# Quarter swaps of convolution weights as DMA transfers, and a re-ordered preparation cycle

## The chip, the cores and the metric

The kernel runs on one core of one Trainium2 chip. The metric is the device time of one execution in microseconds (us). TensorE (PE in the profile) multiplies, VectorE (DVE), ScalarE (ACT) and GpSimd (POOL) work on elements, and SyncE (SP) issues nearly all of the DMA transfers, one after the other from a single queue.

## The reference, cut to what matters

Four residual layers work on x of shape (4, 32, 32, 16): two position-dependent convolutions, one interval-pooling layer, and one more convolution of the same kind. Each normalizes its input first (`_gn`). The time goes to the three convolutions:

```python
first = jnp.einsum('ijyx,byxc->bijc', Msq, inputs)
kern = jnp.transpose(G, (0, 1, 5, 4, 2, 3)).reshape(h * w * f, c, 3, 3)
shifted = lax.conv_general_dilated(x_nchw, kern, (1, 1), 'SAME')   # h*w*f output channels
diff = jax.nn.relu(inputs[:, None, None, :, :, :] - shifted)
second = jnp.einsum('ijyx,bijyxc->bijc', Wsq, diff)
return first - second
...
x = x + _L0_conv_ref(_gn(x), L0_conv_M, L0_conv_W, L0_conv_G)
```

Every output position (i, j) and feature f has its own 3x3x16 kernel in G, so the convolution has 32 * 32 * 16 output channels, and its result is consumed at once by the relu and the weighted sum.

## The kernel before, in words

**Phases, chunks, steps.** Three convolution layers times two pairs of images make six phases. A phase has eight chunks of 128 output positions, a chunk 32 steps (16 features times 2 images), so there are 1,536 steps. A step is a group of matmuls into a pair of PSUM banks, a scaling of them by ScalarE (L663), more matmuls, and one VectorE instruction that applies the relu, multiplies with W and sums (L680). The matmuls of a step are split: `first_part` of step S is issued before `second_part` of step S-1.

**Units.** Weights come in units of four features (`FU`), 192 units u in all, each used by eight steps: unit u is first used at step 8u. To keep fp32 precision on the matmul path, a weight is split into a high part (its upper bits) and a low part. A prepared unit is a tile `parts` of 128 partitions x 2 x 3 x 512 elements: `WU`, `WL`, `WD` for slot 0, and the same three for slot 1, which is slot 0 with its upper and lower 64 partitions exchanged. A second tile, `W9`, holds the ninth tap. There are three buffers of each (`AHEAD + 1`) and two of the raw weights (`RAWS`). The first two units go another way (`prep_plain`).

**Preparation.** The generator `prep_parts` prepares one unit per cycle of eight steps; each `yield` ends a step. For unit u: VectorE masks the raw weights to the high part (`upper`, L203); ScalarE makes `W9` (L175), `WD` (L236) and `WU` (L240); GpSimd subtracts to get `WL` (L237), adds to `W9` (L238) and `WD` (L241), swaps quarters of 32 partitions with four copies (L243, L245), and then subtracts the identity tap from the next unit's raw weights (`prep(u + 1)`, L214), in place. Two transfers from SBUF to SBUF (L251) fill slot 1 from slot 0; the text calls these two the exchange. Then `load_raw` (L110) fetches the raw weights of unit u + 2.

**Other work in the same queues.** The generator `behind` runs what the next phase needs: the norm (`group_norm`), eight small transfers of the normalized image to DRAM (xs<-xt, L381), 24 that read it back as shifted rows (raw<-xs, L392), and `place`, a block of 12 transfers for each of two images (L298, L300), called a placing block here. In the middle of the run it also runs the interval layer. What a step of `prep_parts` yields says whether `behind` may go on in it where it asks for an `IDLE` or a `CALM` step.

**What sets the order.** The schedule is manual: each engine runs its instructions in the order in which the program issues them, and waits on semaphores for data. SP too: a transfer that has to wait holds all that were issued behind it. In `conv_layer`, each step first takes one step of `prep_parts`, then issues its matmuls, and then, if allowed, one piece of `behind`.

Of the kernel before, what the change touches and what calls it, by code (L numbers as in the profile page):

```python
# [8 lines left out]
F32 = mybir.dt.float32  # L9
F32R = mybir.dt.float32r  # L10
I32 = mybir.dt.int32
AF = mybir.ActivationFunctionType
ALU = mybir.AluOpType
AX = mybir.AxisListType

P = 128
# [5 lines left out]
NP = H * H  # L22
# [11 lines left out]
FU = 4  # L34
# [3 lines left out]
HIGH = -(1 << 12)  # L38
# [6 lines left out]
def net_kernel(ctx: ExitStack, tc: tile.TileContext, x, xq, xi, convs, iv_w, iv_b, out):  # L45
# [26 lines left out]
    nc = tc.nc  # L72
    ctx.enter_context(tc.manual_schedule())

    const = ctx.enter_context(tc.tile_pool(name="const", bufs=1))
    wpool = ctx.enter_context(tc.tile_pool(name="wpool", bufs=2))
    work = ctx.enter_context(tc.tile_pool(name="work", bufs=1))
# [20 lines left out]
    IDLE = 0  # L98
    CALM = -1
# [6 lines left out]
    def load_raw(u):  # L106
        if u < n_chunks * NU:
            n = u // NU
            raws[u] = wpool.tile([P, 3, FU, P], F32, tag="raw", bufs=RAWS, name=f"raw_{u}")
            nc.sync.dma_start(raws[u], convs[phases[n // NT][1]][2][n % NT, u % NU])  # L110
# [55 lines left out]
    def rows_mask(name, view):  # L166

        m = const.tile([P, 2], F32, name=name)
        nc.vector.tensor_reduce(m[:, 0:1], view, axis=AX.XYZ, op=ALU.add)
        nc.vector.tensor_scalar(m[:, 1:2], m[:, 0:1], -2.0, 1.0, op0=ALU.mult, op1=ALU.add)  # L170
        return m


    def halve(dst, src, mask):
        nc.scalar.activation(dst, src, AF.Copy, scale=mask[:, 1:2])  # L175
# [18 lines left out]
    QUARTERS = [(slice(64 * h, 64 * h + 32), slice(64 * h + 32, 64 * h + 64)) for h in range(2)]  # L194
# [4 lines left out]
    def upper(src, n, name):  # L199

        t = work.tile([P, 2, NH], F32, tag="upper", bufs=2, name=f"upper_{name}")[:, :n]
        t = t.rearrange("p s (y x) -> p s y x", x=src.shape[3])
        nc.vector.tensor_scalar(  # L203
            t.bitcast(I32), src.bitcast(I32), HIGH, None, op0=ALU.bitwise_and
        )
        return t.rearrange("p s y x -> p s (y x)")

    def prep(u, at=0, to=FU, eng=nc.gpsimd):

        if u >= n_chunks * NU:  # L210
            return
        f0 = u % NU * FU
        for s in range(2 if u < PLAIN else 1):
            eng.tensor_tensor(  # L214
                raws[u][:, s, at:to], raws[u][:, s, at:to],
                pick[s][:, f0 + at : f0 + to].unsqueeze(2).to_broadcast([P, to - at, P]),
                ALU.subtract,
            )

    def prep_parts():  # L220

        for u in range(PLAIN, n_chunks * NU):
            parts = wpool.tile([P, 2, 3, FU, P], F32R, tag="parts", bufs=AHEAD + 1, name=f"parts_{u}")
            W9 = wpool.tile([P, FU, P], F32R, tag="W9", bufs=AHEAD + 1, name=f"W9_{u}")
            units[u] = [parts[:, :, k] for k in range(3)] + [W9]
            src = raws.pop(u)
            w8 = src[:, 0].rearrange("p f k -> p (f k)")  # L230
            WU, WL, WD = (parts[:, 0, k].rearrange("p f k -> p (f k)") for k in range(3))
            high = upper(src[:, 0:1], 1, f"w{u}")[:, 0]
            yield (IDLE,)
            halve(W9, src[:, 1], low_w)
            yield ()
            nc.scalar.activation(WD, high, AF.Copy, scale=-EPS)  # L236
            nc.gpsimd.tensor_tensor(WL, w8, high, ALU.subtract)  # L237
            nc.gpsimd.tensor_tensor(W9, W9.bitcast(F32), src[:, 2], ALU.add)  # L238
            yield ()
            nc.scalar.copy(WU, high)  # L240
            nc.gpsimd.tensor_tensor(WD, WD.bitcast(F32), WL.bitcast(F32), ALU.add)  # L241
            for lo, hi in QUARTERS:
                nc.gpsimd.tensor_copy(WU[hi], WL[lo].bitcast(F32))  # L243
            for lo, hi in QUARTERS:
                nc.gpsimd.tensor_copy(WL[lo], high[hi])  # L245
            yield ()
            prep(u + 1)
            yield (IDLE,)
            yield (IDLE, CALM)
            for h in range(2):  # L250
                nc.sync.dma_start(  # L251
                    parts[64 * h : 64 * h + 64, 1].bitcast(F32),
                    parts[64 - 64 * h : 128 - 64 * h, 0].bitcast(F32),
                )
            load_raw(u + RAWS)
            yield (IDLE, CALM)
            yield (IDLE, CALM)

    def prep_plain(u, at=0, to=FU, eng=nc.gpsimd):
        if at == 0:  # L260
            units[u] = [None] * 3 + [
                wpool.tile([P, FU, P], F32R, tag="W9", bufs=AHEAD + 1, name=f"W9_{u}")
            ]
        prep(u, at, to, eng)
        halve(units[u][3][:, at:to], raws[u][:, 2, at:to], low_p)
# [546 lines left out]
    low_w = rows_mask("low_w", ident.rearrange("p (h w k) -> p w h k", h=2, w=2)[:, 1:2])  # L812
# [6 lines left out]
    nc.vector.tensor_copy(mean_own, ps[:, :1])  # L819
    nc.vector.tensor_scalar_sub(XQ, XQ, mean_own)  # L820
    s2 = const.tile([P, 1], F32, name="s2")
    squares = const.tile([P, 256], F32, name="squares")
    nc.vector.scalar_tensor_tensor(
        squares, XQ, 1.0, XQ, op0=ALU.mult, op1=ALU.mult, accum_out=s2
    )
# [43 lines left out]
    def rest_of_start():  # L869
# [26 lines left out]
        yield from group_norm(0, "c00", xns[0], 4)  # L896

    parts = prep_parts()
    for phase in range(len(phases)):
        conv_layer(phase, behind(phase))  # L900
# [79 lines left out]
```

## Time and profile before

| what | us |
|---|---|
| median of 3 runs (2477.5 to 2477.88) | 2477.75 |
| profiled execution | 2478.41 |
| its span, first to last instruction | 2476.7 |
| PE busy | 2458.2 |
| DVE busy | 2087.3 |
| ACT busy | 1878.4 |
| POOL busy | 1579.7 |

The granted TensorE clock is 1.000 over the whole span. DMA engines were busy 53.0% of the span with the queue that SP feeds. PE is busy 91.15 us of the first 100 us and between 98.95 and 100 of each later 100 us. The columns of a group line are: line, engine, operation, what it writes and reads, shapes and count, then busy time, mean ns of one, and the idle time before it with what ended it. A line of the timeline has start, duration, engine, line, operation and tiles.

### The profile page before, as it was taken

Reading aid. Unit: us, or ns where it says so; the run is one execution under the profiler, and the core shown is the slowest. Engines: PE = TensorE matmul, PEld = TensorE weight load, DVE = VectorE, ACT = ScalarE, POOL = GpSimd, SP = SyncE. Lnnn points to the kernel's source line nnn. Section 1 sums busy time; section 2 is a strip of 40 time slices with the busy share of each in tenths; the row PEclk is TensorE's granted clock in tenths of the full one; section 3 lists DMA queues with packets and bytes.
Section 4 is the critical chain, followed back from the end, with each engine's and each line's share of the span. In section 5 each row is a group of like instructions: output and inputs, shape, how many; then the busy total and the mean of one; then the engine's idle time right before and its main releaser. Section 6 shows DMA issues by size and latency. Waiting matters only on the chain.

```text
span 2476.7 us, 58058 instructions
## 1 busy us (share of the span) xinstructions
PE 2458.2 (99%) x21906; PEld 2090.1 (84%) x21906; DVE 2087.3 (84%) x3617; ACT 1878.4 (76%) x2181; POOL 1579.7 (64%) x1750
## 2 busy tenths in 40 slices
PE   8999999999999999999999999999999999999999
PEld 5999888888888888888888988888998888888887
DVE  9888878888888888778898988899889888788887
ACT  4778767787777778777777777787777787677776
POOL 4766655666565657555567777586878676555552
PEclk9999999999999999999999999999999999999999
DMA  6446754466454467644454545574455467554442
GB/s 198 138 137 182 203 155 135 124 182 164 133 143 135 135 168 198 186 116 134 136 145 127 142 124 140 146 196 125 126 138 144 127 181 195 154 148 137 137 137 54
DMA packets 97673, 366.92 MB, mean 148 GB/s; under 512 B 26480, under 2 KB 31472, under 8 KB 97392
## 3 DMA queue, kind: packets, MB, share of 16 engines
q1 hardware_dynamic: 96832, 362.79, 53.0%
q8 instruction: 172, 2.82, 0.5%
q14 instruction: 109, 0.89, 0.1%
q10 hardware_dynamic: 432, 0.39, 0.1%
q0 software_dynamic: 128, 0.02, 0.0%
HBM read 199.78 MB, written 1.02 MB: 81 GB/s over the span
## 4 chain that ended last, share of the span: by engine, by line
PE 94%; DVE 2%; issue 1%; DMA 1%; ACT 0%; SPq 0%; POOL 0%; ACTq 0%; DVEq 0%; POOLq 0%
PE pc L627 93%; DVE junk L680 1%; PE pf L425 1%; DMA raw<-in_g 1%; ACT pc L663 0%; DMA first<-in_g 0%; SPq L298 0%; DVE raw L846 0%; SPq L300 0%; PE ps_l L548 0%; PE ps_r L561 0%; DMA parts<-parts 0%; DVE tables L508 0%; DVE raw L854 0%; DMA ib<-first 0%
## 5 line engine op out<-in xcount | busy, mean ns | idle before, releaser
L680 DVE SCALAR_TENSOR_TENSOR junk<-pc,WT 128x1024 f32<-128x1024 f32 x1536 | 1879.5, 1224 | 359.1 <-PE pc L627 308.3
L663 ACT ACTIVATE pc<-pc 128x1024 f32<-128x1024 f32 x1520 | 1532.0, 1008 | 561.0 <-PE pc L627 535.8
L627 PE MATMUL pc<-ib,parts 64*128 64x512 f32 x6080 | 958.5, 388 | 4.1 <-DVE junk L680 3.4
L627 PE MATMUL pc<-iyz,parts 64*128 64x512 f32 x6080 | 955.5, 387 | 2.2 <-ACT pc L663 2.0
L627 PE MATMUL pc<-ia,parts 64*128 64x496 f32 x6080 | 933.5, 379 | 0.0
L627 PEld LDWEIGHTS pc<-ia,parts 64*128 64x128 f32 x6080 | 595.5, 184 | 100.8
L627 PEld LDWEIGHTS pc<-ib,parts 64*128 64x128 f32 x6080 | 591.5, 184 | 105.0 <-DVE junk L680 9.9
L627 PEld LDWEIGHTS pc<-iyz,parts 64*128 64x128 f32 x6080 | 592.5, 184 | 88.4 <-ACT pc L663 6.4
L627 PE MATMUL pc<-im,W 64*128 64x496 f32 x3072 | 611.5, 384 | 0.0
L237 POOL TENSOR_TENSOR parts<-raw,upper_w 128x512 fp32r<-128x512 f32 x190 | 248.5, 1308 | 500.2 <-DVE upper_w L203 434.8
L627 PEld LDWEIGHTS pc<-im,W 64*128 64x128 f32 x3072 | 303.0, 184 | 54.5 <-issue 3.2
L243 POOL CAST parts<-parts 32x512 fp32r<-32x512 f32 x380 | 231.1, 608 | 50.1 <-ACT parts L240 31.8
L238 POOL TENSOR_TENSOR W<-W,raw 128x512 fp32r<-128x512 f32 x190 | 247.6, 1303 | 1.8 <-ACT W L175 1.8
L241 POOL TENSOR_TENSOR parts<-parts 128x512 fp32r<-128x512 f32 x190 | 246.8, 1299 | 2.0 <-ACT parts L236 1.9
L245 POOL CAST parts<-upper_w 32x512 fp32r<-32x512 f32 x380 | 231.6, 609 | 22.8
L214 POOL TENSOR_TENSOR raw<-raw,ident 128x512 f32<-128x512 f32 x190 | 199.9, 1052 | 52.2 <-DMA raw<-in_g 28.7
L175 ACT ACTIVATE W<-raw,low_w 128x512 fp32r<-128x512 f32 x190 | 136.2, 717 | 0.1
L680 DVE DVE_READ_ACCUMULATOR junk<-pc,WT 128x1 f32 x1536 | 127.5, 83 | 0.0
L236 ACT ACTIVATE parts<-upper_w 128x512 fp32r<-128x512 f32 x190 | 118.8, 625 | 6.6 <-DVE upper_w L203 6.4
L240 ACT CAST parts<-upper_w 128x512 fp32r<-128x512 f32 x190 | 116.5, 613 | 0.0
L695 POOL TENSOR_SCALAR acc<-acc 128x32 f32<-128x32 f32 x40 | 16.4, 409 | 141.7 <-DVE junk L680 139.7
L203 DVE TENSOR_SCALAR upper_w<-raw 128x512 int32<-128x512 int32 x190 | 86.1, 453 | 1.2 <-POOL raw L214 0.9
(139 smaller groups left out, 479.4 us busy)
## 6 DMA issues: line engine op xcount, KB each, us to landing
raw<-in_g SPq DMA_DIRECT2D x190, 768.0 KB, 7.1
parts<-parts SPq DMA_DIRECT2D x380, 384.0 KB, 4.9
WT<-in_w SPq DMA_DIRECT2D x48, 512.0 KB, 4.6
MT<-in_mt SPq DMA_DIRECT2D x24, 512.0 KB, 7.4
raw<-xs SPq DMA_DIRECT2D x120, 71.8 KB, 2.9
ib<-temp SPq DMA_DIRECT2D x40, 128.0 KB, 2.6
ia<-temp SPq DMA_DIRECT2D x80, 62.0 KB, 3.4
ib<-first SPq DMA_DIRECT2D x8, 128.0 KB, 2.4
```

What stands on the lines that cost most here:

```text
L175: nc.scalar.activation(dst, src, AF.Copy, scale=mask[:, 1:2])
L214: eng.tensor_tensor(raws[u][:, s, at:to], raws[u][:, s, at:to], pick[s][:, f0 + at : f0 + to].unsqueeze(2).to_broadcast([P, to - at, P]), ...
L236: nc.scalar.activation(WD, high, AF.Copy, scale=-EPS)
L237: nc.gpsimd.tensor_tensor(WL, w8, high, ALU.subtract)
L238: nc.gpsimd.tensor_tensor(W9, W9.bitcast(F32), src[:, 2], ALU.add)
L240: nc.scalar.copy(WU, high)
L241: nc.gpsimd.tensor_tensor(WD, WD.bitcast(F32), WL.bitcast(F32), ALU.add)
L243: nc.gpsimd.tensor_copy(WU[hi], WL[lo].bitcast(F32))
L245: nc.gpsimd.tensor_copy(WL[lo], high[hi])
L627: nc.tensor.matmul(ps[:, h, at : at + n], lhsT=w[r], rhs=v[r] if n == NH else v[r][:, :n], start=first and k == 0, stop=k == len(pairs) - ...
L663: nc.scalar.activation(ps, ps, AF.Copy, scale=1.0 + EPS)
L680: nc.vector.scalar_tensor_tensor(junk, ps.rearrange("p h n -> p (h n)"), 0.0, chunks[n], op0=ALU.min, op1=ALU.mult, accum_out=accs[phase][ ...
```

## The change

The four quarter copies leave GpSimd and become four transfers that SP issues. Those that write `WU` are issued one step after the raw load, those that write `WL` two steps later. The exchange of a unit is now issued in the second step of the next unit's cycle (by the new function `exchange`). In GpSimd's cycle the subtraction for the next unit comes first, before `WL`. The mask moves to the second step of the cycle and gets a buffer pair of its own; it now stands seven steps behind the subtraction it needs, where it stood four. The raw load is issued in the fifth step, not in the seventh. The values yielded change accordingly, so `behind` may go on in other steps than before. A 256-element scratch tile (`squares`) moves from the constants to a work buffer.

```diff
+    def exchange(parts):
+        if parts is not None:
+            for h in range(2):
+                nc.sync.dma_start(
+                    parts[64 * h : 64 * h + 64, 1].bitcast(F32),
+                    parts[64 - 64 * h : 128 - 64 * h, 0].bitcast(F32),
+                )
...
+        swapped = None
         for u in range(PLAIN, n_chunks * NU):
...
-            high = upper(src[:, 0:1], 1, f"w{u}")[:, 0]
+            halve(W9, src[:, 1], low_w)
+            yield (CALM,)
+            high = work.tile([P, FU * P], F32, tag="high", bufs=2, name=f"high_{u}")
+            nc.vector.tensor_scalar(
+                high.bitcast(I32), w8.bitcast(I32), HIGH, None, op0=ALU.bitwise_and
+            )
+            exchange(swapped)
             yield (IDLE,)
-            halve(W9, src[:, 1], low_w)
-            yield ()
+            prep(u + 1)
             nc.scalar.activation(WD, high, AF.Copy, scale=-EPS)
             nc.gpsimd.tensor_tensor(WL, w8, high, ALU.subtract)
+            yield (CALM,)
+            nc.scalar.copy(WU, high)
             nc.gpsimd.tensor_tensor(W9, W9.bitcast(F32), src[:, 2], ALU.add)
-            yield ()
-            nc.scalar.copy(WU, high)
+            yield (CALM,)
             nc.gpsimd.tensor_tensor(WD, WD.bitcast(F32), WL.bitcast(F32), ALU.add)
-            for lo, hi in QUARTERS:
-                nc.gpsimd.tensor_copy(WU[hi], WL[lo].bitcast(F32))
-            for lo, hi in QUARTERS:
-                nc.gpsimd.tensor_copy(WL[lo], high[hi])
-            yield ()
-            prep(u + 1)
-            yield (IDLE,)
-            yield (IDLE, CALM)
-            for h in range(2):
-                nc.sync.dma_start(
-                    parts[64 * h : 64 * h + 64, 1].bitcast(F32),
-                    parts[64 - 64 * h : 128 - 64 * h, 0].bitcast(F32),
-                )
             load_raw(u + RAWS)
             yield (IDLE, CALM)
+            for lo, hi in QUARTERS:
+                nc.sync.dma_start(WU[hi].bitcast(F32), WL[lo].bitcast(F32))
             yield (IDLE, CALM)
+            yield (IDLE, CALM)
+            for lo, hi in QUARTERS:
+                nc.sync.dma_start(WL[lo].bitcast(F32), high[hi])
+            swapped = parts
+            yield (IDLE, CALM)
+        yield (IDLE, CALM)
+        exchange(swapped)
...
-    squares = const.tile([P, 256], F32, name="squares")
+    squares = work.tile([P, NP], F32, tag="junk", name="squares")[:, :256]
```

## The prediction, made before the changed kernel was run

> **What bounds the kernel now.** I read the page's busy shares and chain first, then the groups and DMA issues, then the timeline engine by engine in one quiet cycle and in three crowded stretches.
>
> ```profile
> PE 2458.2 (99%) x21906; PEld 2090.1 (84%) x21906; DVE 2087.3 (84%) x3617; ACT 1878.4 (76%) x2181; POOL 1579.7 (64%) x1750
> ...
> PE 94%; DVE 2%; issue 1%; DMA 1%; ACT 0%; SPq 0%; POOL 0%; ACTq 0%; DVEq 0%; POOLq 0%
> ...
> L243 POOL CAST parts<-parts 32x512 fp32r<-32x512 f32 x380 | 231.1, 608 | 50.1 <-ACT parts L240 31.8
> ...
> L245 POOL CAST parts<-upper_w 32x512 fp32r<-32x512 f32 x380 | 231.6, 609 | 22.8
> ...
> raw<-in_g SPq DMA_DIRECT2D x190, 768.0 KB, 7.1
> parts<-parts SPq DMA_DIRECT2D x380, 384.0 KB, 4.9
> ...
> ia<-temp SPq DMA_DIRECT2D x80, 62.0 KB, 3.4
> ```
>
> TensorE is busy 2458.2 of 2476.7 us and is 94% of the chain. POOL, whose four casts per unit go away, is busy 64% and is no part of the bound. So nothing taken off POOL shortens the run by itself; what matters is whether the weights of a unit still arrive before TensorE asks for them. One quiet cycle shows today's margin (POOL, then SP, then PE):
>
> ```profile
> 708.98 1.29 POOL L237 TENSOR_TENSOR parts<-raw,upper_w 128x512 fp32r<-128x512 f32 x1 [4.81 <-DVE upper_w L203]
> ...
> 714.30 1.28 POOL L245 CAST parts<-upper_w 32x512 fp32r<-32x512 f32 x2
> ```
> ```profile
> 715.60 1.10 SPq L251 DMA_DIRECT2D parts<-parts  x2
> 716.81 1.14 SPq L110 DMA_DIRECT2D raw<-in_g  x1
> ```
> ```profile
> 730.51 0.62 PE L627 MATMUL pc<-ib,parts 64*128 64x512 f32 x4
> ```
>
> Unit 56 is masked until 708.84, POOL is done at 715.6, the second exchange lands at 721.2, and its first matmul comes at 730.51: 9.3 us of margin. A step is 1.567 us, a cycle eight steps, 12.54 us. The margin is thinnest where other transfers stand in SP's queue. At the start (SP, then PE):
>
> ```profile
> 34.16 1.19 SPq L251 DMA_DIRECT2D parts<-parts  x2
> 35.39 1.21 SPq L110 DMA_DIRECT2D raw<-in_g  x1
> 36.69 3.33 SPq L298 DMA_DIRECT2D ia<-first  x4
> 40.08 1.29 SPq L300 DMA_DIRECT2D ib<-first  x2
> 41.42 5.84 SPq L298 DMA_DIRECT2D ia<-first  x4
> 47.31 1.29 SPq L300 DMA_DIRECT2D ib<-first  x2
> 48.71 1.17 SPq L251 DMA_DIRECT2D parts<-parts  x2
> ```
> ```profile
> 43.33 0.64 PE L627 MATMUL pc<-ib,parts 64*128 64x512 f32 x4
> ```
>
> and before the last layer, where unit 124 keeps 0.8 us (landing 1599.5, use 1600.3):
>
> ```profile
> 1581.78 5.26 SPq L381 DMA_DIRECT2D xs<-xt  x8
> 1587.82 5.70 SPq L392 DMA_DIRECT2D raw<-xs  x12
> 1593.68 1.11 SPq L251 DMA_DIRECT2D parts<-parts  x2
> ```
>
> **What the Trainium skill says.** "DMA: Bandwidth & Descriptors", section "Queues, rings and completion order": on one engine descriptors are consumed in ring order. The trace agrees: a 62 KB transfer issued at 1617.07, 0.63 us behind a raw load, landed 7.0 us later, 0.3 us after that load. Its section "Two DMAs through the same engine are not ordered": a dependent transfer must wait for the first one's semaphore. The trace agrees: the second raw<-xs is issued at 1588.56, when the last xs<-xt lands (1588.55). "SBUF — State Buffer", section "Who interferes with whom": a VectorE instruction with two SBUF inputs contends with a GpSimd one that reads SBUF. The trace agrees: at 1316.4 a scan (L527) took 1.55 us beside L214, which took 1.83; apart, 1.21 and 1.04.
>
> **The change part by part.** I call a cycle's eight steps A to H and count from the unit's first use, step 8u.
>
> Removed: four casts, 2 x 0.608 + 2 x 0.609 = 2.43 us of POOL per unit. They lay beside TensorE: worth nothing in quiet stretches. In the interval stretch (windows 1200 to 2000) TensorE has 7070 matmuls where eight quiet windows hold 8 x 898 = 7184, so up to 114 / 8.98 = 13 us is lost there, mostly to VectorE's own queue (L508, L527, L680 in the chain). I take 1 us back; bounds 0 and 13.
>
> Moved with one answer: the subtraction (L214) now stands before WL in POOL's queue and needs the raw load, issued a cycle earlier; the load lands well before. The mask moves from A to B, one step (1.57 us) later. Its own buffer pair is read last by the H transfers, ten steps before its reuse. Net 0. The smaller constant tile moves addresses; no row shows a cost, I take 0.
>
> The new chain of a unit, laid over unit 56: mask ends 710.41; WL 1.30 and W9 1.30 behind it end at 713.2; the raw load issues then (1.15). Its landing alone isn't shown, since today it runs behind the exchange. From landings: an exchange DMA issued at 703.07 lands at 706.81, its twin 1.84 later, the load 2.28 after that. So about 1.9 fixed + 2.3 = 4.2 us; bounds 3.7 and the least measured, 5.3. The WU quarters issue at 714.4 to 715.5, land behind the load at 717.6. The WL quarters overwrite what those read, so SP waits: issue 717.7 to 718.8, and with 2.0 us to landing (the nearest row, ia<-first, 62 KB, has 1.9 to 2.0 in a free queue) they land at 720.3. The exchange waits for them: 720.4, its second DMA 720.9 + 5.1 = 726.0. Margin 4.5 us instead of 9.3. SP is held about 8 of 12.54 us. Quiet cycles lose nothing.
>
> Where SP is late the margin is less. Three DMA groups now each wait in SP's one queue, and whatever the program issues between them delays the exchange. I followed the yields of both generators to get SP's order.
>
> - Start: both versions have the first placing block (to 34.1), then today's exchange of unit 2, its load and the second placing block. New: first block, load (34.2), WU quarters, WL quarters (wait for the load, to about 39.4), second block of 12 x 0.64 = 7.7 us to 47.2, and only then, at step 12 instead of 9, the exchange: 47.3 + 5.6 = 52.9. TensorE wants it at 43.3: 9.6 late. The stall of 0.62 at 49.9 for the second block goes, so +9.
> - Placing blocks (L298, L300), two in each of five phases: in the new order all ten stand between a unit's WU quarters or WL quarters and its exchange. 715.6 + 7.7 = 723.3; WL quarters land 725.9; exchange 726.0, lands 731.6: 1.1 late. The next unit starts with SP still behind: about 2.4. Per phase 3.5, times 5: 17.5.
> - xs/raw transfers, first three such phases: the eight xs<-xt leave SP 7.4 us after their step, the quarters follow with two raw<-xs (0.47 each) per step: exchange lands about 1.6 late, once each: 5.
> - The same in the two phases before the last layer: 24 raw<-xs in six steps, all between mask and exchange of units 123 and 155. xs<-xt end at -13.2 from the use; 8 raw<-xs and the load to -7.3; WU quarters -6.1; 8 more -2.3; WL quarters -1.2; 8 more +2.6; exchange lands at +8.3; without the 1.3 us that xs<-xt took beyond eight issues of 0.49, +7.1. I take 7.75 each: 15.5.
> - Elsewhere (norms on POOL, loads of MT and WT in the ring): bounds 0 and 8, since most lateness there stays under 4.5: +1.
>
> Sum: 9 + 17.5 + 5 + 15.5 + 1 - 1 = +47. The profiled execution has 2478.41 (span 2476.7 and 1.7 around it), 0.7 over the median 2477.75; on the median 2525.
>
> **Rivals.** (1) SP catches up: the waits overlap with issue, placing blocks cost nothing, and only the start (9) and the last-layer blocks (about 11) remain: 2498. For it: ty and tz are ready early, two placing DMAs were issued at 224 to 225, long before their step. Against: in one queue early issue still holds the exchange. (2) Every cycle is late: if the quarters land 2.5 us later than a free queue's and the load at 5.3, the 4.5 us are gone and each of 190 units loses; at 0.4 us, with the blocks, 2600. Against: SP and the ring are free by then in quiet cycles. (3) Faster: POOL's absence frees VectorE's shared port, all 13 us of the interval stretch come back, and the exchange waits cost 5 only: 2470. It decides if the quarters' waits are shorter than the blocks' slack, that is, if an exchange issued up to 9 steps before use were not moved behind the blocks. Against: the chain there names VectorE's queue; and at the start the order alone makes 9. (4) The change doesn't do what it says: the casts stay hidden and the transfers too, +-0: 2478. Against: 9.3 us of margin shrink by half on paper.
>
> **How the numbers follow.** Forecast 0.72, rival 1 0.14, rival 2 0.05, rival 3 0.04, rival 4 0.05. A difference under 0.2% (5 us) is what a measurement here can't tell from none. Range: the forecast's sum with placing blocks at 5 to 30, last-layer blocks at 8 to 20, the start at 8 to 14, gives 2495 to 2550; to leave out no more than 2 in 10 with rival 1 inside, 2492 to 2555. Faster 0.04, same 0.05, slower 0.91.
>
> **What would show it.** Right: no cast rows; PE idle time before pc<-ib released by the transfer parts<-parts, some 9 us near 43 to 53, 7 to 8 us once before each of the last two phases, 1 to 3 us in pairs at the placing blocks; quiet windows still 898 matmuls; SP waiting on its own quarter transfers. Wrong: idle time in every cycle (rival 2), no wait on parts<-parts (rivals 3, 4), or another count than 898 in quiet windows, which would mean that addresses matter.

## The result and the profile after

The kernel after takes 2627.09 us (median of 5 runs, 2622.19 to 2629.08), the one before 2477.75. Over all runs the ratio is 1.0598, with a 95% interval of 1.0583 to 1.0614. By the medians that is 149 us slower, where 47 were forecast. The span of the profiled execution grew from 2476.7 to 2620.5 us, by 143.8. The page of after, in the rows that answer to those shown of before:

```profile
PE 2523.5 (96%) x21906; PEld 2223.5 (85%) x21906; DVE 2087.0 (80%) x3617; ACT 1882.0 (72%) x2181; POOL 1109.9 (42%) x990
...
PE 74%; DMA 10%; DVE 4%; SPq 4%; issue 3%; POOL 2%; ACT 2%; DVEq 0%; ACTq 0%; POOLq 0%
...
L638 PE MATMUL pc<-ib,parts 64*128 64x512 f32 x6080 | 1046.0, 393 | 74.3 <-DMA parts<-parts 68.5
...
raw<-in_g SPq DMA_DIRECT2D x190, 768.0 KB, 5.2
parts<-parts SPq DMA_DIRECT2D x380, 384.0 KB, 4.8
...
parts<-parts SPq DMA_DIRECT2D x380, 64.0 KB, 4.7
parts<-high SPq DMA_DIRECT2D x380, 64.0 KB, 2.0
```

POOL did lose 470 us of work, and the run got no shorter for it. TensorE's idle time ahead of the matmuls that read `parts` rose from 4.1 to 74.3 us, ended by transfers for 68.5; the chain has 10% of DMA where it had 1%. But TensorE is also *busy* for 65 us more, with the same 21,906 matmuls. That is the first sign of something the forecast had no term for.

A quiet cycle, SP's timeline of after (start, duration, line, tiles):

```profile
807.52 0.33 SPq L110 DMA_DIRECT2D raw<-in_g  x1
807.95 1.18 SPq L260 DMA_DIRECT2D parts<-parts  x2
812.37 1.73 SPq L264 DMA_DIRECT2D parts<-high  x2
815.51 1.14 SPq L223 DMA_DIRECT2D parts<-parts  x2
820.12 0.33 SPq L110 DMA_DIRECT2D raw<-in_g  x1
```

This is the chain of the forecast: load, WU quarters (L260), a wait until they have landed, WL quarters (L264), a wait, exchange (L223). TensorE doesn't stop here. The waits of SP, over the whole span of after (total, times, longest):

```profile
SPq L264 <- DMA parts<-parts: 658.6, 182, 6.0
SPq L110 <- POOL W L254: 341.5, 141, 6.5
SPq L223 <- DMA parts<-high: 259.9, 176, 2.9
```

The first and the third row are SP waiting for its own quarter transfers: 918 us of the span, with every other transfer queued behind. The sum alone says little, for before had SP wait longer still for what its exchange reads, and TensorE hardly stopped:

```profile
SPq L251 <- ACT parts L240: 855.6, 159, 13.1
SPq L251 <- POOL parts L245: 539.2, 164, 8.3
```

What is new is that three groups of transfers now wait on each other, late in the cycle, with less margin behind them. Where others are queued between them, TensorE stops. Before the last layer, SP and then TensorE (in brackets the idle time before the matmul and what ended it):

```profile
1669.27 1.18 SPq L260 DMA_DIRECT2D parts<-parts  x2
1670.51 4.47 SPq L403 DMA_DIRECT2D raw<-xs  x8
1675.08 1.15 SPq L264 DMA_DIRECT2D parts<-high  x2
1676.27 3.85 SPq L403 DMA_DIRECT2D raw<-xs  x8
1680.17 1.14 SPq L223 DMA_DIRECT2D parts<-parts  x2
```
```profile
1677.32 1.13 PE L638 MATMUL pc<-ib,parts 64*128 64x512 f32 x2 [2.47 <-DMA parts<-high]
1683.98 0.79 PE L638 MATMUL pc<-ib,parts 64*128 64x512 f32 x1 [5.54 <-DMA parts<-parts]
```

At the start the same thing happens to unit 2: SP has the exchange at 49.16, after the second placing block, and TensorE stands still for 8.71 us until 53.09:

```profile
49.16 1.23 SPq L223 DMA_DIRECT2D parts<-parts  x2
```
```profile
53.09 0.79 PE L638 MATMUL pc<-ib,parts 64*128 64x512 f32 x1 [8.71 <-DMA parts<-parts]
```

I aligned the two traces at the first pc<-ib matmul of each step; the growth of the difference over a stretch of steps is what that stretch lost:

| stretch (steps) | forecast, us | lost, us | TensorE idle in it | lost to half clock |
|---|---|---|---|---|
| start (to 96) | 9 | 14.1 | 11.3 | 2.6 |
| xs/raw transfers, first three phases (96 to 128, 288 to 320, 544 to 576) | 5 | 21.8 | 11.7 | 7.3 |
| placing blocks (128 to 192, 320 to 352, 576 to 624, 1000 to 1016, 1250 to 1280) | 17.5 | 56.9 | 31.7 | 16.2 |
| xs/raw before the last layer (976 to 1000, 1232 to 1250) | 15.5 | 26.6 | 18.5 | 6.5 |
| interval stretch (768 to 976, 1016 to 1232) | -1 | 13.3 | 8.3 | 0 |
| all other steps | 1 | 11.1 | 2.8 | 0 |
| sum | 47 | 143.8 | 84.3 | 32.6 |

The two last columns don't make up the whole. Before was idle for 6.3 us in the same steps, so 78 us of the 143.8 are idle time and 32.6 half clock. The other 33 us are TensorE busy for longer at full clock with the same matmuls: 13 of them in steps beside a stop or in part at half clock, 20 elsewhere.

The last column is the second loss. TensorE's timeline of after, at unit 14's stop:

```profile
208.81 0.39 PE L638 MATMUL pc<-ib,parts 64*128 64x512 f32 x2
213.10 0.79 PE L638 MATMUL pc<-ib,parts 64*128 64x512 f32 x1 [3.91 <-DMA parts<-parts]
215.04 0.79 PE L638 MATMUL pc<-ib,parts 64*128 64x512 f32 x1 [1.15 <-DMA parts<-parts]
...
217.31 0.63 PE L638 MATMUL pc<-ib,parts 64*128 64x512 f32 x1
...
219.87 0.82 PE L638 MATMUL pc<-ib,parts 64*128 64x512 f32 x4
...
221.49 0.78 PE L638 MATMUL pc<-ib,parts 64*128 64x512 f32 x4
```

The weights are there at 215.04, yet the last 11 of that step's 14 matmuls take 2.27 us, and the whole step that begins at 217.31 takes 2.56 instead of 1.57; the one at 219.87 takes 1.62 again: the trace's clock record has 0.5 of full speed from 212.5 to 219.4. The window of 100 us around it (busy time and count of PE and the other engines; then the granted clock) shows it as 0.91:

```profile
200.00:300.00 100.00, 87.65 (x700) 77.84 (x698) 66.88 (x111) 63.97 (x75) 42.62 (x37) 0.91 0.65 172
```

Before had full clock wherever its weights were used. After has 14 such pieces, 88.7 us in all. The matmuls in each, at 1.567 us for a step's 14, would have taken less than its busy time by 32.6 us together.

### The profile page after: what moved, and what is told of

Read it like the earlier page. It is cut to its first block, busy times and chain, and to the rows that moved or that the text cites. A ratio compares the mean times of both kernels' runs of the same rounds, so it can differ in the third digit from the quotient of the medians.

```text
span 2620.5 us, 58906 instructions
## 1 busy us (share of the span) xinstructions
PE 2523.5 (96%) x21906; PEld 2223.5 (85%) x21906; DVE 2087.0 (80%) x3617; ACT 1882.0 (72%) x2181; POOL 1109.9 (42%) x990
## 4 chain that ended last, share of the span: by engine, by line
PE 74%; DMA 10%; DVE 4%; SPq 4%; issue 3%; POOL 2%; ACT 2%; DVEq 0%; ACTq 0%; POOLq 0%
PE pc L638 73%; DMA parts<-parts 6%; DVE junk L691 3%; DMA raw<-in_g 2%; ACT pc L674 1%; DMA parts<-high 1%; SPq L403 1%; PE pf L436 1%; SPq L309 1%; POOL W L254 1%; POOL parts L251 1%; SPq L264 1%; DVE high L244 1%; DMA ia<-temp 0%; SPq L311 0%
## 5 line engine op out<-in xcount | busy, mean ns | idle before, releaser
L674 ACT ACTIVATE pc<-pc 128x1024 f32<-128x1024 f32 x1520 | 1531.5, 1008 | 670.3 <-PE pc L638 647.7
L638 PE MATMUL pc<-ib,parts 64*128 64x512 f32 x6080 | 1046.0, 393 | 74.3 <-DMA parts<-parts 68.5
L638 PE MATMUL pc<-iyz,parts 64*128 64x512 f32 x6080 | 1031.4, 393 | 10.0 <-ACT pc L674 8.9
L638 PE MATMUL pc<-ia,parts 64*128 64x496 f32 x6080 | 1012.3, 384 | 0.0
L638 PEld LDWEIGHTS pc<-ib,parts 64*128 64x128 f32 x6080 | 672.6, 186 | 162.7 <-DMA parts<-parts 86.7
L638 PEld LDWEIGHTS pc<-ia,parts 64*128 64x128 f32 x6080 | 675.4, 187 | 68.0
L638 PE MATMUL pc<-im,W 64*128 64x496 f32 x3072 | 673.1, 388 | 0.0
L214 POOL TENSOR_TENSOR raw<-raw,ident 128x512 f32<-128x512 f32 x190 | 199.8, 1052 | 654.1 <-DMA raw<-in_g 500.2
L251 POOL TENSOR_TENSOR parts<-raw,high 128x512 fp32r<-128x512 f32 x190 | 247.1, 1300 | 408.7 <-DVE high L244 317.8
L250 ACT ACTIVATE parts<-high 128x512 fp32r<-128x512 f32 x190 | 119.2, 627 | 36.4 <-DVE high L244 33.6
L253 ACT CAST parts<-high 128x512 fp32r<-128x512 f32 x190 | 116.0, 610 | 0.0
L244 DVE TENSOR_SCALAR high<-raw 128x512 int32<-128x512 int32 x190 | 93.1, 490 | 0.2
```

What stands on the lines that cost most here:

```text
L214: eng.tensor_tensor(raws[u][:, s, at:to], raws[u][:, s, at:to], pick[s][:, f0 + at : f0 + to].unsqueeze(2).to_broadcast([P, to - at, P]), ...
L244: nc.vector.tensor_scalar(high.bitcast(I32), w8.bitcast(I32), HIGH, None, op0=ALU.bitwise_and)
L638: nc.tensor.matmul(ps[:, h, at : at + n], lhsT=w[r], rhs=v[r] if n == NH else v[r][:, :n], start=first and k == 0, stop=k == len(pairs) - ...
L674: nc.scalar.activation(ps, ps, AF.Copy, scale=1.0 + EPS)
```

## The experiments

Ratios are over all runs, against before timed beside each of them on the same chip, with 95% intervals; before was at 2477.6 to 2480.0 there.

**Whose transfers delay the exchange?** *no_other_transfers*: after, without the transfers that `behind` issues from the second layer on: this edit for xs<-xt and raw<-xs, and a like one in `place`.

```diff
-            for h in range(2):
+            for h in range(2 if layer == 0 else 0):
```

> The changed kernel, which from the second layer on leaves out the placing transfers and the xs<-xt and raw<-xs transfers (images of the first layer stay in place, so values differ from there on). Theory (what stands in SP's queue ahead of a unit's three waiting groups makes TensorE stop): the stops from unit 38 on go, save those beside MT loads; what stays are the start and units 14 to 20 (37 us), the interval stretch (13) and small ones: about 2535 us. Rival (the quarter transfers' own waits and traffic): over 2600 us.

Measured 2537.91 us, 1.0249 (1.0231 to 1.0268). From step 288 to 624, where after lost 39.2 us, 1.7 are lost; in steps 976 to 1016, 22 became none, and in 1232 to 1280, 22 became 1. TensorE's row in this run's page:

```profile
L638 PE MATMUL pc<-ib,parts 64*128 64x512 f32 x6080 | 990.7, 389 | 26.2 <-DMA parts<-parts 25.5
```

What stays is the start and the first phase's transfers (36 us), which this run keeps, the interval stretch (14), and 7.5 in all other steps. So the chain of waits in SP's queue stops next to nothing in these stretches by itself; it takes other transfers in that queue. Whether it takes the chain too is asked below.

*placing_spread*: after, each placing block from the second phase on spread over six steps, two transfers in each.

```diff
                 for to, src in ((lo, ty), (hi, tz)):
                     nc.sync.dma_start(da[to, s, :LAST], src[lo, s, at : at + LAST])
+                if spread_out:
+                    yield 1
...
```

> The changed kernel, with each placing block's twelve transfers issued two per step over six steps instead of all in one step. Theory: WL quarters and the exchange get in between, so the stops at units 17, 18, 42, 43, 74, 75, 125, 126, 157 and 158 (30 us idle, some 16 us of half clock) go, others stay: about 2580 us. Rival (ring traffic of the placing transfers, not the order, is what delays the exchange): no gain, 2620 us or more.

Measured 2609.60, 1.0526 (1.0509 to 1.0544): 18 us regained of the 47 expected. The stops at units 17, 43, 75, 125 and 157 went or shrank, but smaller ones came at their neighbours (units 44 to 46, 78 to 82, 127, 159): the placing stretches lost 23.6 us instead of 56.9, all the others together 15 more. I take it that what doesn't stand in one cycle's queue stands in the next one's; no run tests that by itself. Idle time fell only from 84.7 to 79.2 us; half clock from 88.7 to 61.4.

**Which part of the edit costs what?** *exchange_late_only*: before, with the exchange alone moved to the second step of the next unit, three steps later.

```diff
             halve(W9, src[:, 1], low_w)
+            exchange(swapped)
             yield ()
...
-            for h in range(2):
-                nc.sync.dma_start(
...
             load_raw(u + RAWS)
+            swapped = parts
```

> The kernel before with one part of the change: the exchange is issued in the second step of the next unit's cycle. Theory (order in SP's queue): the start stops about 10 us (with half clock 13 more than before), unit 124 and 156 about 6 us each (9 with half clock), second placing blocks about 1 us each: about 2515 us. Rival (the re-ordered GpSimd cycle, not the exchange, makes the 71 us of the variant with copies): under 2490 us.

Measured 2529.22, 1.0203 (1.0188 to 1.0218): 52 us with not one transfer added, and so without the chain of quarter transfers. TensorE's waits for the exchange (total, times, longest):

```profile
PE pc L635 <- DMA parts<-parts: 33.2, 18, 5.6
```

34.1 us ran at half clock. The interval stretch lost only 1.6. So stops don't need the chain of waits either: an exchange issued three steps later, with others' transfers ahead of it, is enough.

*swaps_in_gpsimd*: after, the quarter copies back on GpSimd in the steps where after issues transfers, the rest of the new order kept.

```diff
-                nc.sync.dma_start(WU[hi].bitcast(F32), WL[lo].bitcast(F32))
+                nc.gpsimd.tensor_copy(WU[hi], WL[lo].bitcast(F32))
...
```

> The changed kernel with its new order, but the quarter swaps are GpSimd copies again. Theory (order in SP's queue: each of the three waiting DMA groups can be held by other transfers): no wait for quarters is left, only the late exchange. Placing blocks and the first three xs blocks stop nothing; the start stops about 5.5 us and each of the two 24-transfer blocks before the last layer about 5.5 us, so idle TensorE time about 25 us with the start's usual 6, half clock after three stops, about 2505 us. Rival (the new cycle's order on GpSimd, or the moved addresses, are the cause): still above 2590 us.

Measured 2549.85, 1.0286 (1.0269 to 1.0303): neither side. Nearly half of the loss is there without the transfers. The stops at units 2, 14, 123 and 155 (3.6 to 6.7 us idle each) wait for the exchange, as those of exchange_late_only do, and the interval stretch loses 14.8.

*unchained_quarters*: after with the same number and sizes of transfers, but no group reads or overwrites what the one before it handles; the exchange copies from the unit before (its edit is left out here).

```diff
-                nc.sync.dma_start(WL[lo].bitcast(F32), high[hi])
+                nc.sync.dma_start(WL[hi].bitcast(F32), high[lo])
```

> The changed kernel with as many transfers of the same sizes, but not one after the other: the second pair writes WL's other quarters, which nothing reads meanwhile, and the exchange copies the unit before (values differ). Theory (the waits for landing, which hold SP, are what the four transfers cost): the exchange is issued 3 to 5 us earlier, margin in quiet cycles 6 to 7 us, about 2550 us, as with the copies on GpSimd. Rival (their number, issue time and ring traffic): 2610 us or more.

Measured 2579.22, 1.0409 (1.0394 to 1.0425), between the two. SP's waits for its own quarters are gone; it now waits most for the buffer of the raw load:

```profile
SPq L110 <- DVE high L245: 699.1, 161, 13.3
```

Against after, the waits of the quarter transfers thus cost 48 us. Against swaps_in_gpsimd, the four transfers cost some 30 by being there. That second figure is rougher, since the exchange waits for the copies in the one run and for no quarters in the other; whether it is their issue or the traffic that costs isn't told apart.

*swaps_by_dma_old_order*: before, with the four copies replaced by four transfers on the spot.

```diff
-                nc.gpsimd.tensor_copy(WU[hi], WL[lo].bitcast(F32))
+                nc.sync.dma_start(WU[hi].bitcast(F32), WL[lo].bitcast(F32))
...
```

> The kernel before with nothing changed but the four copies, which become four transfers at the same place in the program. Theory: the exchange stands before the placing blocks as it did, waits for WL quarters about 2.6 us longer, margin in quiet cycles about 6.5 us; stops of about 2 us before each of the last two phases; about 2484 us. Rival (the quarter transfers themselves are too slow for a cycle, or slow TensorE by contention): margin under 3 us in quiet cycles, or over 2550 us.

Measured 2620.26, 1.0561 (1.0540 to 1.0582), where I had expected almost nothing. Its waits of SP, of GpSimd, and of VectorE for its mask:

```profile
SPq L243 <- ACT parts L240: 652.5, 144, 13.6
SPq L245 <- DMA parts<-parts: 363.0, 195, 6.0
SPq L251 <- DMA parts<-upper_w: 226.8, 175, 3.0
```
```profile
POOL raw L214 <- DMA raw<-in_g: 532.3, 146, 13.2
```
```profile
DVE upper_w L203 <- DMA parts<-upper_w: 24.7, 7, 6.3
DVE upper_w L203 <- POOL raw L214: 17.9, 16, 3.7
```

The raw load still stands behind all three groups and comes late, and GpSimd's subtraction waits for it (28.7 us in before, 532.3 here). That wait alone shows little: after has 500.2 us of it, with the mask seven steps behind the subtraction. Here the mask follows after four, and waits for the subtraction and for quarter transfers that still read the buffer it is to write, where before waited 0.9 us for the subtraction. In after the mask waits for neither (its idle time is 0.2 us in all). So the earlier load, the later mask and the mask's own buffers fit together as an answer to these waits; which of them is needed was not tested one by one. The new order is not simply a mistake beside the transfers, and it has its own price. The parts don't add up.

*exchange_at_once*: after, with the exchange right behind the WL quarters.

```diff
-            swapped = parts
+            exchange(parts)
```

> The changed kernel, with the exchange issued right behind the WL quarters in the same step instead of two steps later. Theory: the start's exchange stands before the second placing block again and its stop falls from 8.7 to about 3 us; before the last layer eight raw<-xs fewer stand ahead of it, stops 9 to about 5 us each; placing blocks issued between WU and WL quarters stay as they are: about 2600 us. Rival (SP's own hold of 2 us while the quarters land costs as much elsewhere): 2627 us, as the changed kernel.

Measured 2646.81, 1.0673 (1.0655 to 1.0691): slower still. The stops I had aimed at shrank (TensorE's idle time at units 123 and 155 from 9.0 and 9.4 to 8.0 and 7.9 us, at unit 2 from 9.7 to 4.0), but units 71, 74, 125 and 157 now stop for 3.9 to 5.4 us, where after had 0.6 to 4.1, and 102.4 us ran at half clock. SP's wait for the WL quarters' landing now stands in the step that issues them, with `behind`'s transfers waiting; its sum rises only from 259.9 to 295.1 us, so that this is the cause is not shown.

**What does one stop cost?** *stall_ladder*: before, with the exchange of twelve units (`HELD`) delayed by chains of 4 to 10 small transfers, each of which overwrites what the last one read; these units' raw load goes ahead of the chain.

```diff
+            held = HELD.get(u, 0)
+            for k in range(held):
+                nc.sync.dma_start(
+                    zero[:, WP * (k % 2) : WP * (k % 2) + WP],
+                    zero[:, WP * (1 - k % 2) : WP * (1 - k % 2) + WP],
+                )
```

> The kernel before, where twelve units in quiet stretches have their exchange held by a chain of 4 to 10 small transfers (each waits for the one before it), the raw load issued first. It measures what one stop of TensorE costs. From the margin of 9.3 us, 4.3 us for the load and 1.95 per link: stops of about 2, 4, 6, 8, 10 and 14 us for 4, 5, 6, 7, 8 and 10 links, 78 us idle in all. Theory (a stop also leaves TensorE at half clock for a while): about 3 us more for each, none or half of it for the shortest: about 2590 us. Rival (a stop costs its idle time alone): about 2556 us.

Measured 2502.26 (two runs), 1.0097 (1.0077 to 1.0117). The holds were shorter than I had reckoned, and only four units stopped. They still give the price. Unit 95's stop:

```profile
1242.40 0.50 PE L638 MATMUL pc<-ib,parts 64*128 64x512 f32 x1 [3.70 <-DMA parts<-parts]
1244.27 0.79 PE L638 MATMUL pc<-ib,parts 64*128 64x512 f32 x1 [1.37 <-DMA parts<-parts]
```

Units 87 and 95: 8.1 us idle, 15.1 lost, 13.65 us at half clock. Unit 180: 2.3 idle, 4.7 lost, 3.41 at half clock. Unit 60: 0.5 idle, 1.0 lost, no half clock. So a stop of 2 to 5 us costs 2.4 to 3.6 us more than its length, and a short one next to nothing more. Of the 9.4 us that the three long stops cost beyond their length, half clock makes 6.8. (3.5 us were also lost at the start, where nothing was held; I have no cause for that.)

**Why does the interval stretch lose 13 us?** Two runs on after with GpSimd's copies, and with the exchange back in its own cycle, one step later than before. (The expectation counts two steps for this delay and five for that of after; by the edits they are one and three.)

*order_only*:

```diff
             for lo, hi in QUARTERS:
-                nc.sync.dma_start(WL[lo].bitcast(F32), high[hi])
-            swapped = parts
+                nc.gpsimd.tensor_copy(WL[lo], high[hi])
+            exchange(parts)
```

> After with the four quarter copies on GpSimd and the exchange issued in their own cycle, right behind the last copy (step H), so that no transfer is added and the exchange is two steps later than before instead of five. Theory (it is the exchange that comes late in SP's queue, the re-ordered cycle itself costs only the interval stretch its 13 to 15 us): about 2500, interval stretch again 6 to 8 us over in each of its two halves, stops over 4 us only at unit 2 or none. Rival (the re-order itself costs most of what swaps_in_gpsimd lost): 2540 or more.

Measured 2530.77, 1.0200 (1.0182 to 1.0218): the rival is nearer. Most of what swaps_in_gpsimd lost is lost here too, 14.9 of it in the interval stretch.

*order_only_calm_as_before*: the same, with the interval's scans allowed in three of eight steps, as in before.

```diff
-            yield (CALM,)
+            yield ()
```

> order_only, but the interval's scans are allowed in the same three of eight steps as before, not in seven. Theory (the interval stretch loses because scans now fall in steps in which VectorE has the mask and the halving of W9, a matter of VectorE's queue): 12 us less than order_only, with the interval stretch within 2 us of before. Rival (the loss there comes from the new place of GpSimd's subtraction beside the scans): same time as order_only within 4 us.

Measured 2538.99, 1.0239 (1.0223 to 1.0255): 8 us worse, 18.0 lost in the interval stretch. So the steps in which the scans may run are not the cause. ScalarE's waits are, as the next two runs show. In after, its row for `WD` (L250), then a piece of its timeline:

```profile
ACT parts L250 <- DVE high L244: 33.6, 47, 4.3
```
```profile
1480.01 1.01 ACT L674 ACTIVATE pc<-pc 128x1024 f32<-128x1024 f32 x1 [0.59 <-PE pc L638]
1482.25 0.63 ACT L250 ACTIVATE parts<-high 128x512 fp32r<-128x512 f32 x1 [1.23 <-DVE high L244]
1482.79 1.00 ACT L674 ACTIVATE pc<-pc 128x1024 f32<-128x1024 f32 x1
```

`WD` reads the mask. In before the mask was issued two steps ahead of it (A and C) and the wait came 5 times, 6.4 us in all; now it is issued one step ahead (B and C). The mask stands in VectorE's queue behind instructions that themselves wait for TensorE, so `WD` waits, and behind `WD` stands the scaling of pc (L674), for which TensorE waits. TensorE's weight loads show that wait in after:

```profile
PEld pc L638 <- ACT pc L674: 30.6, 58, 1.6
```

Both waits in before:

```profile
ACT parts L236 <- DVE upper_w L203: 6.4, 5, 2.8
```
```profile
PEld pc L627 <- ACT pc L663: 6.4, 11, 0.8
```

Two runs move only the mask and the halving of W9.

*order_only_mask_at_a* and *mask_at_a*: order_only and after, with mask and halving of W9 exchanged.

```diff
-            halve(W9, src[:, 1], low_w)
-            yield (CALM,)
             high = work.tile([P, FU * P], F32, tag="high", bufs=2, name=f"high_{u}")
             nc.vector.tensor_scalar(
                 high.bitcast(I32), w8.bitcast(I32), HIGH, None, op0=ALU.bitwise_and
             )
+            yield (CALM,)
+            halve(W9, src[:, 1], low_w)
```

> order_only with the same exchange of mask and halving. Theory: waits of WD on the mask from 44.7 to under 10 us, the interval stretch within 3 us of before, the small stops at a unit's step 5 gone; 20 us less than order_only, about 2510, and what remains is the exchange two steps late. Rival: 2525 or more.

> After with mask and halving of W9 exchanged, so that the mask is again in step A, two steps ahead of ScalarE's WD that reads it, with everything else as in after. Theory (WD stands ahead of the eviction of pc in ScalarE's queue; one step behind the mask, it waits for VectorE's queue, 33.6 us in 47 waits in after's profile, and TensorE then waits for the eviction): waits of WD on the mask back to some 6 us, the interval stretch within 3 us of before, the run 12 to 20 us less than after, about 2610; the stops on parts<-parts remain. Rival (the loss of the interval stretch comes from GpSimd's or the transfers' place): the time of after within 5 us.

Measured 2511.16, 1.0125 (1.0110 to 1.0141), 20 us less than order_only, with 0.5 lost in the interval stretch; and 2615.46, 1.0556 (1.0538 to 1.0573), against after's 1.0598 some 10 us less, with 2.4 lost there. Of the latter run, ScalarE's and the weight loads' waits:

```profile
ACT parts L250 <- DVE high L242: 4.3, 2, 2.3
```
```profile
PEld pc L638 <- DMA parts<-parts: 93.9, 50, 8.2
...
PEld pc L638 <- ACT pc L674: 6.0, 11, 0.8
```

The waits on the mask are gone and those on the transfers are not: two causes, told apart. In mask_at_a the second is a little larger than in after (86.7), and the xs/raw stretches lose 7.5 us more, which goes with its regaining 10 and not 20.

No run was as fast as before. Before has 6.3 us of TensorE idle time after its first 14 us, so an order without the late exchange has little to win.

## Why the prediction was right or wrong

**Right: the mechanism and the places.** GpSimd was not the bound, and 470 us less of its work bought nothing. The chain in SP's queue came out as laid over unit 56, and every place named lost time: the start, placing blocks in pairs, the xs/raw blocks, most before the last layer. The run without other transfers shows that they are what delays the exchange in the later phases. At the start I had the exchange 9.6 us late; TensorE's gaps there are 8.71 and 1.01.

**Wrong: the sum.** The forecast's 47 us are idle time alone. The 143.8 are 78 of idle time, 31 more than forecast, 32.6 at half clock and 33 of slower work at full clock; the last two had no term at all. Four steps of the sum failed.

- *No term for the clock.* Each stop was priced at its length. Of the 143.8 us, 32.6 are matmuls at half clock after the stops, and the ladder shows the surcharge by itself. The Trainium skill has it ("TensorE: Matmul & The Clock Gate", section "Why this matters for your kernels"): it advises against TensorE gaps of more than about 3 us, since a window of idle time brings the clock down. The trace agrees, with 3.41 to 13.65 us at half clock at each stop of over 2.3 us, and goes further (below).
- *The sizes of the stops.* The quiet margin was put at 4.5 us; in the quiet stretches it has a median of 3.75 (9.3 in before), over all units 3.2. From the issue of the load the exchange lands after 13.6 us in the cycle at 807.5, where my steps add up to 12.8: the WL quarters took 3.1 instead of 2.6, the wait for the WU quarters 0.4 more. With less margin, and with units after a late one starting late as well, placing blocks kept TensorE idle for 31.7 us (17.5 forecast) and the first three xs/raw blocks for 11.7 (5 forecast). The last-layer blocks were nearest: 18.5 against 15.5. That placing blocks could reach 30 was in the range as a bound; beside everything else it was not enough. (The range's lower end was added up wrongly, the three lower bounds give 2504 and not 2495; the miss is at the other end.)
- *"The mask moves from A to B, one step (1.57 us) later", and "Net 0".* I looked at who reads the buffer last, not at who waits for the mask: `WD`, now one step behind it, with TensorE's eviction queued behind `WD`. Worth 10 us in after, 20 with the copies on GpSimd. My -1 for the interval stretch came out as +13.3; with the mask back at A it is 2.4. Of the 33 us of slower work at full clock, 22 stay in mask_at_a.
- *"Elsewhere", +1.* It was 11.1, of which 7.0 are in steps 624 to 656 and 1280 to 1344 (the stretches with the MT loads) and 4.1 in the quiet stretches. TensorE is idle for 2.8 of the 11.1; most of the rest is again slower work at full clock.

**Quiet cycles** don't stop, as forecast, but their windows have 890 to 895 matmuls and not 898: slower work at full clock, and part of the 33 us. I had named a changed count as a sign that addresses matter. The run exchange_at_once, with the same tiles, has 1.567 us for a step in the same stretches, and mask_at_a has it in two of three; so it isn't the addresses alone, and the cause stays open. Over whole runs this slower work is 6 to 7 us in the two runs with the mask at A and no added transfer (exchange_late_only, order_only_mask_at_a), and 22 and 30 in two with the mask at A and the four transfers (mask_at_a, swaps_by_dma_old_order). It goes with the transfers and their stops; how is not shown.

**The rivals.** The first (SP catches up, 2498), the third (faster) and the fourth (no effect) fall with the stops that are there. The second (2600) came nearest in time by another way than its own: no loss in every cycle, but more at the places named. Of what the edit consists of, the late exchange alone costs 52 us, more than I gave the whole; with the re-ordered cycle 71, with four unchained transfers 101, with their waits 149. This is one path of several: the re-ordered cycle with the exchange only one step late costs 51 by itself (order_only).

## What to carry to other kernels

When work moves from an idle engine into a queue that issues for everybody, count what else stands in that queue and for how long each new wait holds it; a transfer that waits for the transfer before it costs its landing, not its issue. Price a stop of TensorE at its length plus the clock it loses, and look for the slack of every consumer of a moved instruction, not only of its buffer: one step less between a producer and an in-order engine's reader can stop what is queued behind that reader. A margin in the quiet part of a run says little about the crowded parts.

## What the runs showed of the hardware

**Half clock after short gaps.** I took the gaps of TensorE after 30 us in after and all twelve experiments, joined those less than 4 us apart, and looked for half clock within 5 us of each group. Of 68 groups with 0.8 to 1.2 us of gaps none was followed by it, of 33 with 1.2 to 1.6 us three, of 26 with 1.6 to 2.0 nine, of 15 with 2.0 to 2.3 ten, and of 97 with more than 2.3 us all. The figure of about 3 us in the Trainium skill ("TensorE: Matmul & The Clock Gate", section "Why this matters for your kernels") is thus too generous here: two gaps of 1.2 and 1.1 us, less than 4 us apart, were enough in after at 1042.4, and one of 1.88 us in swaps_in_gpsimd at 257.0. The pieces are always a multiple of 3.41 us, one to four of them.

**Eight transfers of SP under way, by the program.** In after the load issued at 197.48 had seven transfers behind it by 201.56; SP's next one went out at 204.64, and the load had landed at 204.63. In none of the 14 traces was one of SP's transfers issued before the one eight issues back had landed. The trace names a reason: SP's transfers take eight completion semaphores in turn, and the one at 204.64 waits for the semaphore that the load raises. So this limit is the program's, and no run here shows one of the hardware. It held SP for some 27 us in after and 37 in before, so it is no part of what after lost.
